# Two graph-attention layers with experts and a recurrence: the graph cast to bytes by DRAM-to-DRAM transfers, in place of int32 loads and casts on GpSimd

## The chip, the cores and the metric

The kernel runs on one core of a Trainium2 chip, a trn2. A core has four compute engines: TensorE (PE; its weight loads are shown as PEld), VectorE (DVE), ScalarE (ACT) and GpSimd (POOL). Each takes its own queue of instructions in order. A fifth queue, SyncE (SP), issues transfers. Sixteen transfer engines, shared by all queues, move the data. Transfers are issued from SP, ACT or POOL. Engines and transfers wait for each other through semaphores.

The metric is the device time of the whole program in microseconds (us). Less is better.

## What is computed

There are 3327 tokens of 256 features, and a dense graph `adj` of 3327 x 3327 int32 values, each 0 or 1. Only the parts around the change are shown in full:

```python
# layer 0: attention over the graph, 2 heads of 128
W3h = (h @ W3.T + b3).reshape(n, HEADS, C)
s1, s2 = ...                        # two scores for each token and head
e = leaky_relu(s1[:, None, :] + s2[None, :, :], 0.2)
e = where(adj[:, :, None] == 1, e, NEG)
att = softmax(e, axis=1)
h_prime = einsum('ijh,jhc->ihc', att, W3h)
# layer 0: the two best of 16 experts for each token
# layer 1: attention over the same graph, 1 head of 256, then elu
# layer 1: 30 steps of h + 0.01 tanh(h), h sigmoid(h), layernorm, h @ W.T + b
```

Both attention layers use the same graph. Each layer normalizes its input, and adds its result to it.

## The kernel before

**Tiles.** The 3327 tokens make NT = 26 tiles of up to 128, or PAIRS = 13 pairs. Token 2p + b of a pair stands at partition p of tile b of the pair. NP = 26 x 128 = 3328, so there is one place without a token: the last partition of tile 25. `rows(t)` gives the tokens of a tile: 128, and 127 for the last one.

**The graph in memory.** `adjT` holds the transposed graph as one-byte floats. [...]two neighbouring tokens travel together, and the tile is seen both as `adj_pairs` (two-byte) and as `adjT` (bytes). One tile of 128 rows of the graph fills the columns of `adjT` that belong to these 128 query tokens, for all tokens that they may attend to.

**Filling it** (`transpose_graph`, L240 to L264). For each of the 26 tiles, SP loads the rows in two halves of int32 into `raw` (three buffers), GpSimd casts each half to bytes in `bytes` (two buffers; L263, 52 casts in all), and a DMA transpose from SP (L264) writes them into `adj_pairs`. GpSimd also clears the column without a token (L262) and the last partitions of tile 25 (L260).

**The order of work at the start.** The weights of layer 0 are loaded by seven transfers from GpSimd (L319, L331). `project` (L130) goes over the tokens in seven groups (six of four tiles, one of two). For a group, `normalized` (L103) takes mean and variance on DVE, the reciprocal root on GpSimd (`rstd`, L114), and scales on DVE (`xn`, L116). Then, for two tiles at a time, PE transposes (L126), ACT copies (L127), PE multiplies by the weights (L141), and `split0` writes `wh`, the values that are to be averaged, and the scores. After `project` come, in program order, `transpose_graph` for all tiles, the loads of `gate_w` and `gate_b` from GpSimd (L365, L366), four small tables made by GpSimd (L368 to L377) and `before` (L378), which the routing to experts needs.

**Attention** (`attend`, L163). The query tiles are taken in groups: in layer 0 of 4, 6, 6, 6 and 4 tiles (`groups0`), in layer 1 of 3. One group and one head make a part, ten parts in layer 0. In a part the loop goes over the 26 tiles j of tokens that are attended to. In each step ACT makes `e` (L212), DVE adds and multiplies by the bytes of the graph (`pT`, L217), and PE multiplies `pT` by `wh[:, j]` for each tile of the group (L222, each matmul as two instructions in the trace). `wh` has a last column of ones, so the row sums come out of the same product. When a part is done, `close` divides (L195, L384) in the steps of the next part, a bit in each step. After the second head, `route` (L391) of that group is worked off in the same manner: normalize (with `rstd` on GpSimd), write `x` to `acc` and the normalized rows to `table_x` in DRAM (L398, L399, issued by SP), multiply by `gate_w` on PE (L406), find the two best experts on DVE, and scatter places into lists with GpSimd (L473).

**Who sets the order.** The program's lines are put into the five queues by a planner when the program is built. It prefers earlier lines, and takes later ones where earlier ones, by its estimate, can't run yet. Each engine then works its queue in order, and stops at an instruction whose inputs have not arrived.

**After attention 0.** The experts run from about 500 us, layer 1 (which projects with the same `project`, L716) from about 920, and the 30 steps to the end.

Of the kernel before, what the change touches and what calls it, by code (L numbers as in the profile page):

```python
# [17 lines left out]
P = 128  # L18
# [9 lines left out]
def gat_moe_gat_recurrent_ffn(ctx: ExitStack, tc: tile.TileContext, a: dict, out: bass.AP):  # L28
    nc = tc.nc
    N, D = a["x"].shape  # L30
    KD = D // P
    NT = (N + P - 1) // P
    NP = NT * P
    PAIRS = NT // 2
    REST = N - 2 * P * (PAIRS - 1)
    assert NT % 2 == 0
    E = a["gate_w"].shape[1]
    HID = a["w1"].shape[2]
    FH = HID // P
# [7 lines left out]
    def rows(t):  # L47
        return P if t < NT - 2 else (REST + 1 - t % 2) // 2

    def spread(n):  # L50

        cut = n - n % 16
        return [r for r in ((0, cut), (cut, n)) if r[0] < r[1]]
# [41 lines left out]
    neg_half = const.tile([P, MOST], F32, name="neg_half")  # L95
    nc.vector.memset(neg_half, -0.5)

    def load(name, shape, src, q=None):
        t = const.tile(shape, F32, name=name)
        (q or nc.sync).dma_start(t, src)  # L100
        return t

    def normalized(src, dst, scale=1.0):  # L103

        n = len(src)
        mv = small.tile([P, MOST, 2], F32, name="mv")
        for j in range(n):
            st = small.tile([P, 6], F32, name="st")
            nc.vector.bn_stats(st, src[j])
            nc.vector.bn_aggr(mv[:, j, :], st)  # L110
        ve = small.tile([P, MOST], F32, name="ve")
        nc.vector.tensor_scalar(ve[:, :n], mv[:, :n, 1], EPS, 1.0 / scale**2, op0=ALU.add, op1=ALU.mult)  # L112
        r = small.tile([P, MOST], F32, name="rstd")
        nc.gpsimd.tensor_tensor(r[:, :n], ve[:, :n], neg_half[:, :n], ALU.pow)  # L114
        for j in range(n):
            nc.vector.tensor_scalar(  # L116
                dst[j], src[j], mv[:, j, 0:1], r[:, j : j + 1], op0=ALU.subtract, op1=ALU.mult
            )
# [8 lines left out]
        nc.scalar.copy(hT, pt)  # L127
        return hT

    def project(wv, n_out, finish, work, ps, ps_p):  # L130

        for ts in groups:
            n = len(ts)
            xn = work.tile([P, G, D], F32, name="xn")
            normalized([x[:, t, :] for t in ts], [xn[:, j, :] for j in range(n)])
            for j0 in range(0, n, 2):
                hT = turned(xn[:, j0 : j0 + 2, :], work, ps)
                for j in range(2):
                    p = ps_p()
                    for k in range(KD):  # L140
                        nc.tensor.matmul(  # L141
                            p[:, :n_out], lhsT=hT[:, j, k, :], rhs=wv[:, k, :], start=(k == 0), stop=(k == KD - 1)
                        )
                    finish(ts[j0 + j], p)
# [92 lines left out]
    adj_pairs = graph.tile([P, PAIRS, NP], BF16, name="adjT")  # L237
    adjT = adj_pairs.bitcast(FP8).rearrange("p c (i b) -> p c i b", b=2)

    def transpose_graph(ts, pools):  # L240

        raw_p, cast_p = pools
        half = NP // 2
        for i in ts:
            pr = rows(i)
            b = cast_p.tile([P, NP], FP8, name="bytes")
            for lo in (0, half):
                real = min(half, N - lo)
                raw = raw_p.tile([P, half], I32, name="raw")
                for r0, r1 in spread(pr):  # L250
                    first = i // 2 * 2 * P + i % 2 + 2 * r0
                    nc.sync.dma_start(
                        raw[r0:r1, :real],
                        bass.AP(
                            tensor=a["adj"].tensor, offset=a["adj"].offset + first * N + lo,
                            ap=[[2 * N, r1 - r0], [1, real]],
                        ),
                    )
                if pr < P:
                    nc.gpsimd.memset(b[96:P, lo : lo + half], 0.0)  # L260
                if real < half:
                    nc.gpsimd.memset(b[:, lo + real : lo + half], 0.0)  # L262
                nc.gpsimd.tensor_copy(b[:pr, lo : lo + real], raw[:pr, :real], saturate=False)  # L263
            nc.sync.dma_start(adj_pairs[:, :, i * P : (i + 1) * P], b.bitcast(BF16), transpose=True)  # L264

# [10 lines left out]
    with ExitStack() as moe:  # L276
# [15 lines left out]
        with ExitStack() as st:  # L292
# [2 lines left out]
            keep = st.enter_context(tc.tile_pool(name="keep0", bufs=1))  # L295
            wh = keep.tile([P, NT, H, C + 1], F32, name="wh")
            sc = Scores(keep, H)
            gpools = (
                st.enter_context(tc.tile_pool(name="raw", bufs=3)),
                st.enter_context(tc.tile_pool(name="cast", bufs=2)),  # L300
            )
            ps = st.enter_context(tc.tile_pool(name="ps0", bufs=4, space=PSUM))
            ps_o = st.enter_context(tc.tile_pool(name="ps0o", bufs=2, space=PSUM))
            nc.vector.memset(wh[:, :, :, C : C + 1], 1.0)
# [4 lines left out]
            with ExitStack() as pre:  # L309
# [48 lines left out]
                    if t % G == G - 1 or t == NT - 1:  # L358
                        sc.finish(t - t % G, t + 1)

                project(wv, D + 2 * H, split0, work, ps, bank)
                transpose_graph(range(NT), gpools)


                nc.gpsimd.dma_start(gw, a["gate_w"].rearrange("(k p) e -> p k e", p=P))  # L365
# [25 lines left out]
            def route(ts):  # L391
# [3 lines left out]
                row = gate.tile([P, MOST, D], F32, name="row")  # L395
                normalized([x[:, t, :] for t in ts], [row[:, j, :] for j in range(n)])
                here = slice(t0 * P, (t0 + n) * P)
                nc.sync.dma_start(acc[here, :].rearrange("(t p) d -> p t d", p=P), x[:, t0 : t0 + n, :])  # L398
                nc.sync.dma_start(table_x[here, :].rearrange("(t p) d -> p t d", p=P), row[:, :n, :])  # L399
                yield  # L400
                pg = bank()[:, : n * E].rearrange("p (j e) -> p j e", e=E)
                for j0 in range(0, n, 2):
# [279 lines left out]
    with ExitStack() as st:  # L682
# [31 lines left out]
                sc.finish(t - t % G, t + 1)  # L714

        project(wv, D + 2, split1, work, ps, spot)  # L716

        run = st.enter_context(tc.tile_pool(name="edge2", bufs=3))
        rows_p = st.enter_context(tc.tile_pool(name="rows2", bufs=2))
# [146 lines left out]
```

## Time and profile before

| what | us |
|---|---|
| median of three runs | 2192.99 (2190.41 to 2193.59) |
| the profiled execution's own time | 2196.02 |
| its span, first to last instruction | 2194.3 |
| mean granted TensorE clock of it | 0.974 |

Times in the profile count from the start of the span. An engine's busy time leaves out waiting, and the issue of transfers is not counted as busy. The span and what lies around it make up the execution's own time (1.7 us more). In the profile's groups, a line has the place in the code, the engine and operation, what is written and read with the shape, the count, the busy time in us, the mean of one in ns, and after the second bar how long the engine stood idle just before these instructions, and what released it.

Milestones of this execution, from its timeline:

| event | us |
|---|---|
| first load of the graph issued (L252) | 11.3 |
| first matmul of `project` (L141) | 21.5 |
| first `e` of attention 0 (L212) | 65.1 |
| first matmul with `gate_w` (L406) | 144.6 |
| last cast of the graph (L263) | 236.0 |
| last division of attention 0 (L384) | 465.1 |

### The profile page before, as it was taken

Reading aid. Unit: us, or ns where it says so; the run is one execution under the profiler, and the core shown is the slowest. Engines: PE = TensorE matmul, PEld = TensorE weight load, DVE = VectorE, ACT = ScalarE, POOL = GpSimd, SP = SyncE. Lnnn points to the kernel's source line nnn. Section 1 sums busy time; section 2 is a strip of 40 time slices with the busy share of each in tenths; the row PEclk is TensorE's granted clock in tenths of the full one; section 3 lists DMA queues with packets and bytes.
Section 4 is the critical chain, followed back from the end, with each engine's and each line's share of the span. In section 5 each row is a group of like instructions: output and inputs, shape, how many; then the busy total and the mean of one; then the engine's idle time right before and its main releaser. Section 6 shows DMA issues by size and latency. Waiting matters only on the chain.

```text
span 2194.3 us, 31785 instructions
## 1 busy us (share of the span) xinstructions
PE 2024.3 (92%) x10912; PEld 1685.9 (77%) x10912; DVE 1574.8 (72%) x3948; ACT 1128.2 (51%) x1496; POOL 1030.5 (47%) x744
## 2 busy tenths in 40 slices
PE   5888898957999999869999999999999999999998
PEld 4788898954555555558888888888888888888887
DVE  6889876851121111155767589999999999999999
ACT  1655565721222222245665556666666666666664
POOL 5536402033444443310010027777777777777774
PEclk9989999977999999989999999999999999999999
DMA  9969400015666666320000000000000000000003
GB/s 283 305 209 234 119 15 16 30 39 142 175 186 172 195 177 157 84 82 8 15 8 15 8 32 1 1 1 1 1 1 1 1 1 1 1 1 1 1 1 106
DMA packets 124905, 155.08 MB, mean 71 GB/s; under 512 B 51561, under 2 KB 94637, under 8 KB 124745
## 3 DMA queue, kind: packets, MB, share of 16 engines
q1 hardware_dynamic: 109241, 133.12, 19.8%
q0 software_dynamic: 15360, 19.51, 5.0%
q8 instruction: 87, 1.43, 0.3%
q14 instruction: 73, 0.60, 0.1%
q10 hardware_dynamic: 144, 0.43, 0.0%
HBM read 170.95 MB, written 22.89 MB: 88 GB/s over the span
## 4 chain that ended last, share of the span: by engine, by line
PE 54%; DVE 18%; DMA 11%; issue 8%; POOL 4%; ACT 3%; SPq 2%; another core or an unknown queue 0%; POOLq 0%; DVEq 0%; ACTq 0%
PE po L801 20%; PE acc L222 15%; DVE x L806 5%; DMA raw<-in_adj_dram 5%; PE pa L620 4%; PE pb L620 4%; DVE stats L793 4%; PE po L651 4%; DMA ew<-in_w_dram 4%; PE pt L795 3%; ACT zT L797 3%; DVE v L768 2%; DVE v L767 2%; POOL bytes L263 2%; POOL lists L473 2%
## 5 line engine op out<-in xcount | busy, mean ns | idle before, releaser
L801 PE MATMUL po<-wc,zT 128*128 128x256 f32 x3120 | 705.3, 383 | 22.5 <-ACT zT L797 21.1
L801 PEld LDWEIGHTS po<-wc,zT 128*128 128x128 f32 x3120 | 582.9, 190 | 125.2 <-ACT zT L797 50.8
L222 PE MATMUL acc<-wh,pT 128*128 128x129 f32 (+1 forms) x4056 | 627.9, 316 | 32.1 <-DVE pT L217 27.3
L222 PEld LDWEIGHTS acc<-wh,pT 128*128 128x128 f32 x4056 | 575.5, 195 | 78.5 <-DVE pT L217 36.8
L217 DVE SCALAR_TENSOR_TENSOR pT<-e,part,adjT 128x384 f32<-128x384 f32 (+3 forms) x494 | 417.8, 856 | 152.2 <-PE acc L222 134.9
L212 ACT ACTIVATE e<-rb,minus,full 128x384 f32<-128x384 f32 (+3 forms) x494 | 398.6, 823 | 236.5 <-DVE pT L217 212.9
L787 POOL TENSOR_TENSOR th<-th,x 128x1024 f32<-128x1024 f32 (+1 forms) x210 | 460.5, 2211 | 42.8 <-ACT th L785 37.6
L797 ACT COPY zT<-pt 128x1024 f32<-128x1024 f32 (+1 forms) x210 | 199.4, 949 | 334.2 <-PE pt L795 334.2
L806 DVE SCALAR_TENSOR_TENSOR x<-po,rr,bb 128x256 f32<-128x256 f32 x780 | 323.4, 475 | 0.3 <-PE pt L795 0.3
L776 POOL TENSOR_TENSOR rr<-v,neg_half 128x4 f32<-128x4 f32 (+1 forms) x210 | 203.3, 968 | 216.1 <-DVE v L772 216.1
L793 DVE BATCH_NORM_STATS2 stats<-z 128x6 f32<-128x256 f32 x780 | 282.2, 413 | 0.2 <-ACT z L788 0.2
L114 POOL TENSOR_TENSOR rstd<-ve,neg_half 128x4 f32<-128x4 f32 (+3 forms) x28 | 30.7, 1096 | 433.4 <-DVE ve L112 343.6
L644 DVE TENSOR_TENSOR hid<-act,pb 128x512 f32<-128x512 f32 x67 | 46.1, 688 | 261.9 <-PE pb L620 261.9
L788 ACT ACTIVATE z<-th 128x1024 f32<-128x1024 f32 (+1 forms) x210 | 210.6, 1003 | 0.8 <-DVE stats L793 0.4
L785 ACT ACTIVATE th<-x 128x1024 f32<-128x1024 f32 (+1 forms) x210 | 199.2, 994 | 2.8 <-DVE x L116 1.9
L795 PE MATMUL pt<-ident,z 128*128 128x128 f32 x1560 | 191.6, 274 | 2.5 <-DVE high L727 2.5
L795 PEld LDWEIGHTS pt<-ident,z 128*128 128x128 f32 x1560 | 179.3, 141 | 14.9 <-issue 2.9
L654 POOL DMA_INDIRECT acc<-y,to x67 | 106.0, 1581 | 171.4 <-DMA acc<-y,to 89.4
L768 DVE SCALAR_TENSOR_TENSOR v<-v 128x4 f32<-128x4 f32 (+1 forms) x210 | 157.0, 748 | 0.0
L634 ACT ACTIVATE act<-pa 128x512 f32<-128x512 f32 x67 | 40.0, 597 | 218.7 <-PE pa L620 218.7
L620 PE MATMUL pa<-ew,hT 128*128 128x512 f32 x268 | 129.7, 607 | 17.2 <-DMA ew<-in_w_dram 16.1
L651 PE MATMUL po<-ew,hidT 128*128 128x256 f32 x536 | 126.9, 380 | 0.7 <-ACT hidT L640 0.7
(174 smaller groups left out, 1537.2 us busy)
## 6 DMA issues: line engine op xcount, KB each, us to landing
ew<-in_w_dram SPq DMA_DIRECT2D x201, 512.0 KB
raw<-in_adj_dram SPq DMA_DIRECT2D x25, 832.0 KB
raw<-in_adj_dram SPq DMA_DIRECT2D x25, 831.5 KB
x<-in_x_dram SPq DMA_DIRECT2D x6, 512.0 KB
x<-acc SPq DMA_DIRECT2D x6, 512.0 KB
kept<-x SPq DMA_DIRECT2D x8, 384.0 KB
old<-kept SPq DMA_DIRECT2D x6, 512.0 KB
out_dram<-x SPq DMA_DIRECT2D x6, 512.0 KB
```

Source lines behind the costliest of these rows:

```text
L212: nc.scalar.activation(e[:, : n * P], rb[:, : n * P], AF.Relu, scale=sc.full[:, j, h : h + 1], bias=sc.minus[:, j, h : h + 1],)
L217: nc.vector.scalar_tensor_tensor(pT[:, : n * P], e[:, : n * P], sc.part[:, j, h : h + 1], adjT[:, j // 2, ts[0] * P : (ts[-1] + 1) * P, j ...
L222: nc.tensor.matmul(po[c], lhsT=pT[:, c * P : (c + 1) * P], rhs=wh[:, j, h, :], start=(j == 0 and c % per_bank == 0), stop=(j == NT - 1), s ...
L620: nc.tensor.matmul(p, lhsT=hT[:, k, :], rhs=w[:, k, :], start=(k == 0), stop=(k == KD - 1))
L651: nc.tensor.matmul(po, lhsT=hidT[:, f, :], rhs=w3[:, f, :], start=(f == 0), stop=(f == FH - 1))
L787: nc.gpsimd.tensor_tensor(th[:, :n, :], th[:, :n, :], hs, ALU.add)
L788: nc.scalar.activation(z[:, :n, :], th[:, :n, :], AF.Silu, scale=1.0 / S)
L793: nc.vector.bn_stats(stats[:, j, :], z[:, j, :])
L795: nc.tensor.transpose(pt[:, j, k, :], z[:, j, k * P : (k + 1) * P], ident)
L797: nc.scalar.copy(zT[:, :n, :, :], pt[:, :n, :, :])
L801: nc.tensor.matmul(po[:, j, :], lhsT=zT[:, j, k, :], rhs=wc[:, k, :], start=(k == 0), stop=(k == KD - 1),)
L806: nc.vector.scalar_tensor_tensor(x[:, ts[0] + j, :], po[:, j, :], rr[:, j : j + 1], bb, op0=ALU.mult, op1=ALU.add)
```

## The change

The graph is cast by the transfers. For each pair of tiles, `cast_graph` takes a tile in DRAM of 256 rows of bytes, and GpSimd issues transfers from the int32 graph in DRAM to it, in pieces of at most 2048 columns: two for a pair, and four for the last pair, 28 in all. The generator gives control back after each pair. `project` got a new argument `aside`, and asks it for two pairs behind the `normalized` of each group. `transpose_graph` then issues two DMA transposes for a pair from SP, which read every second row from DRAM. There are 26 transposes as before.

The column without a token is not cleared any more: the pieces read one element past the row's end, which is the first of the next row, and the row of `wh` that it meets is multiplied by 0 instead. `real` is a column of ones with a 0 in the last partition, and it scales tile 25 of `wh`, its ones included, in both layers. The graph's last rows without a token are filled with zeros from SP, from a tile that is there already. The writes of `acc` and `table_x` are issued from ACT instead of SP. The buffers `raw` and `cast` and the unused function `load` go.

```diff
+    real = const.tile([P, 1], F32, name="real")
+    nc.gpsimd.iota(
+        real, pattern=[[0, 1]], base=rows(NT - 1), channel_multiplier=-1, allow_small_or_imprecise_dtypes=True
+    )
+    nc.vector.tensor_scalar(real, real, 0.0, None, op0=ALU.is_gt)
...
-    def project(wv, n_out, finish, work, ps, ps_p):
+    def project(wv, n_out, finish, work, ps, ps_p, aside=iter(())):
...
             normalized([x[:, t, :] for t in ts], [xn[:, j, :] for j in range(n)])
+            for _ in range(2):
+                next(aside, None)
...
-    def transpose_graph(ts, pools):
-
-        raw_p, cast_p = pools
-        half = NP // 2
-        for i in ts:
-            pr = rows(i)
-            b = cast_p.tile([P, NP], FP8, name="bytes")
-            for lo in (0, half):
-                real = min(half, N - lo)
-                raw = raw_p.tile([P, half], I32, name="raw")
...
-                if pr < P:
-                    nc.gpsimd.memset(b[96:P, lo : lo + half], 0.0)
-                if real < half:
-                    nc.gpsimd.memset(b[:, lo + real : lo + half], 0.0)
-                nc.gpsimd.tensor_copy(b[:pr, lo : lo + real], raw[:pr, :real], saturate=False)
-            nc.sync.dma_start(adj_pairs[:, :, i * P : (i + 1) * P], b.bitcast(BF16), transpose=True)
+    def cast_graph(zero, made):
...
+        last = N - 1 - 2 * P * (PAIRS - 1)
+        for c in range(PAIRS):
+            b = dram.tile([2 * P, NP], FP8, name=f"graph{c}")
+            first = 2 * P * c
+            pieces = [(0, 2 * P, N + 1)]
+            if c == PAIRS - 1:
+                pieces = [(0, last, N + 1), (last, last + 1, N)]
+                nc.sync.dma_start(b[last:, :], zero[: 2 * P - last, : NP // 4].bitcast(FP8))
+            for r0, r1, n in pieces:
+                for lo in range(0, n, 2048):
+                    hi = min(n, lo + 2048)
+                    nc.gpsimd.dma_start(
+                        b[r0:r1, lo:hi],
+                        bass.AP(
+                            tensor=a["adj"].tensor, offset=a["adj"].offset + (first + r0) * N + lo,
+                            ap=[[N, r1 - r0], [1, hi - lo]],
+                        ),
+                    )
+            made.append(b)
+            yield
+
+    def transpose_graph(c, b):
+
+        for i in range(2):
+            nc.sync.dma_start(
+                adj_pairs[:, :, (2 * c + i) * P : (2 * c + i + 1) * P],
+                b.bitcast(BF16).rearrange("(p i) n -> i p n", i=2)[i], transpose=True,
+            )
...
-                project(wv, D + 2 * H, split0, work, ps, bank)
-                transpose_graph(range(NT), gpools)
+                in_bytes = []
+                casting = cast_graph(zero, in_bytes)
+                project(wv, D + 2 * H, split0, work, ps, bank, casting)
+                assert len(in_bytes) == PAIRS
+                nc.vector.tensor_scalar(wh[:, NT - 1], wh[:, NT - 1], real[:, 0:1], None, op0=ALU.mult)
+                for c, b in enumerate(in_bytes):
+                    transpose_graph(c, b)
...
-                nc.sync.dma_start(acc[here, :].rearrange("(t p) d -> p t d", p=P), x[:, t0 : t0 + n, :])
-                nc.sync.dma_start(table_x[here, :].rearrange("(t p) d -> p t d", p=P), row[:, :n, :])
+                nc.scalar.dma_start(acc[here, :].rearrange("(t p) d -> p t d", p=P), x[:, t0 : t0 + n, :])
+                nc.scalar.dma_start(table_x[here, :].rearrange("(t p) d -> p t d", p=P), row[:, :n, :])
...
         project(wv, D + 2, split1, work, ps, spot)
+        nc.vector.tensor_scalar(wh[:, NT - 1], wh[:, NT - 1], real[:, 0:1], None, op0=ALU.mult)
```

More of the change, by code (lines that the diff above doesn't have):

```diff
@@ L35, in gat_moe_gat_recurrent_ffn @@
     REST = N - 2 * P * (PAIRS - 1)
-    assert NT % 2 == 0
+    assert NT % 2 == 0 and N == NP - 1
     E = a["gate_w"].shape[1]
@@ L96, in gat_moe_gat_recurrent_ffn @@
     nc.vector.memset(neg_half, -0.5)
[L98 to L101, printed above, removed]
+    real = const.tile([P, 1], F32, name="real")
[3 more added lines that the diff above has]
+    nc.vector.tensor_scalar(real, real, 0.0, None, op0=ALU.is_gt)
     def normalized(src, dst, scale=1.0):
@@ L238, in gat_moe_gat_recurrent_ffn @@
     adjT = adj_pairs.bitcast(FP8).rearrange("p c (i b) -> p c i b", b=2)
-    def transpose_graph(ts, pools):
-        raw_p, cast_p = pools
-        half = NP // 2
-        for i in ts:
-            pr = rows(i)
-            b = cast_p.tile([P, NP], FP8, name="bytes")
-            for lo in (0, half):
-                real = min(half, N - lo)
-                raw = raw_p.tile([P, half], I32, name="raw")
[L250 to L253, printed above, removed]
+    def cast_graph(zero, made):
[12 more added lines that the diff above has]
+                        b[r0:r1, lo:hi],
@@ L254, in transpose_graph @@
                         bass.AP(
-                            tensor=a["adj"].tensor, offset=a["adj"].offset + first * N + lo,
-                            ap=[[2 * N, r1 - r0], [1, real]],
-                        ),
-                    )
-                if pr < P:
-                    nc.gpsimd.memset(b[96:P, lo : lo + half], 0.0)
-                if real < half:
-                    nc.gpsimd.memset(b[:, lo + real : lo + half], 0.0)
-                nc.gpsimd.tensor_copy(b[:pr, lo : lo + real], raw[:pr, :real], saturate=False)
@@ L297, in gat_moe_gat_recurrent_ffn @@
             sc = Scores(keep, H)
[L298 to L301, printed above, removed]
             ps = st.enter_context(tc.tile_pool(name="ps0", bufs=4, space=PSUM))
```

## The prediction

> **What bounds the kernel now.** I read the slices of the page first, then the busy time by stretch inside layer 0, then the queue of GpSimd in order of time, last the transfers. The change lies in the first 465 us. Beyond, only one line of it runs, in layer 1.
>
> ```profile
> PE   5888898957999999869999999999999999999998
> POOL 5536402033444443310010027777777777777774
> DMA  9969400015666666320000000000000000000003
> ```
> A slice is 55 us. TensorE is nearly full throughout; the transfers are full in the first slices, where the graph comes in, and almost idle from slice 5 to 8. The question is whether this early load holds TensorE.
>
> ```profile
> 65.00:129.00 64.00, 55.82 (x446) 52.55 (x445) 59.71 (x63) 45.13 (x61) 30.23 (x26) 0.97 1.07 306
> ...
> 180.00:223.00 43.00, 38.28 (x325) 36.85 (x325) 41.62 (x38) 26.40 (x29) 24.21 (x19) 1.00 1.03 269
> ...
> 272.00:314.00 42.00, 37.15 (x304) 36.71 (x303) 28.91 (x40) 26.61 (x28) 4.94 (x5) 0.92 0.01 1
> 314.00:360.00 46.00, 44.23 (x389) 43.31 (x387) 36.21 (x85) 29.90 (x33) 10.05 (x9) 1.00 0.11 36
> 360.00:402.00 42.00, 36.57 (x293) 36.08 (x292) 27.95 (x38) 25.11 (x26) 4.52 (x5) 0.88 0.01 1
> 402.00:436.00 34.00, 31.27 (x270) 30.18 (x269) 29.34 (x88) 23.15 (x33) 2.50 (x2) 1.00 0.14 48
> 436.00:463.00 27.00, 24.05 (x204) 22.95 (x203) 18.53 (x32) 17.14 (x22) 12.64 (x12) 1.00 0.02 1
> ```
> The columns are length, then busy time of PE, PEld, DVE, ACT, POOL, then clock, DMA share and GB/s. The stretches are the parts of attention 0 (one group of rows, one head), cut where the first closing reciprocal (L195) of a part stands. While the graph comes in, DVE is the full engine (59.7 of 64, 41.6 of 43); afterwards it is not (28.9 of 42), and PE sets the pace. The same L217 is slower beside the casts, here in 160 to 240 and in 280 to 400 us:
>
> ```profile
> L217 DVE SCALAR_TENSOR_TENSOR pT<-e,part,adjT 128x768 f32<-128x768 f32 x48 | 67.6, 1438 | 4.7 <-PE acc L222 4.1 <-ACT e L212 0.6
> ...
> L217 DVE SCALAR_TENSOR_TENSOR pT<-e,part,adjT 128x768 f32<-128x768 f32 x74 | 75.0, 1015 | 26.3 <-PE acc L222 22.7 <-remote 1.7 <-ACT e L212 1.7
> ```
> No wait of DVE is for adjT: the graph itself is in time. That leaves what the new transfers do to GpSimd's queue and to what stands behind them:
>
> ```profile
> 17.54 1.01 POOL L114 TENSOR_TENSOR rstd<-ve,neg_half 128x4 f32<-128x4 f32 x1 [0.83 <-DVE ve L112]
> 18.50 0.10 POOL L262 MEMSET bytes<- 128x1 fp8e4 x1
> 18.54 0.76 POOL L365 DMA_DIRECT2D gate_w<-in_gate_w_dram  x1
> ...
> 22.75 1.04 POOL L114 TENSOR_TENSOR rstd<-ve,neg_half 128x4 f32<-128x4 f32 x1 [1.97 <-DVE ve L112]
> 23.77 1.56 POOL L263 CAST bytes<-raw 128x1664 fp8e4<-128x1664 int32 x1
> ```
> GpSimd's queue is not in program order: gate_w, written after all casts, was put before the first. But the four rstd of groups 0 to 3 (6.94, 12.57, 15.71, 17.54 us) have nothing between them, though the memset was ready: earlier lines that can run go first.
>
> ```profile
> SPq L252 <- DMA lists<-zero: 4.7, 1, 4.7
> SPq L252 <- DMA x<-in_x_dram: 2.5, 1, 2.5
> ```
> These are SP's own waits up to 30 us. The first load of the graph shares no data with lists<-zero, yet waits for it: that was the transfer eight places ahead. The transfers of SP and ACT take eight completion counters in turn, and one is taken again only when its last transfer has landed. GpSimd's have eight of their own: in the records its ninth transfer, gate_b, waits on the counter of the first, gw. So at most eight GpSimd transfers are under way, and the next one stops the whole in-order queue.
>
> **What the Trainium skill says.** "DMA: Bandwidth & Descriptors", section "SWDGE vs HWDGE vs iDMA": a transfer that casts can be issued from GpSimd only; no run shows one yet. Its section "Queues, rings and completion order": each transfer engine takes the descriptors of one ring in order; nothing in the trace contradicts it. Its section "Why a DMA increments its semaphore by 16 and not by 1": the number of engines is the largest divisor up to 16 of the slowest dimension, with an exception for some GpSimd copies; 254 rows would give 2. The trace doesn't show this case. "SBUF — State Buffer", section "Who interferes with whom": a DVE instruction with two SBUF inputs contends with a GpSimd instruction that reads SBUF; the trace agrees, 1438 against 1015 ns.
>
> **Removed: 52 casts on GpSimd.** What they cost is L217's slowing. I compare parts of equal kind: parts 0 and 1 took 64 us; parts 8 and 9 took 61, of which 5 are the route of six tiles (part 6 against part 7, 46 to 42), while the final part closes 2 us earlier: 58, so 6 won. Part 2 took 51, like part 6 with its 46: 5 won, some of it clock (0.87 there). Part 3: 43 against 42, 1. Part 4: 49 against 46, 3. Together 15 us. No more, because PE's 1.37 us a step (12 matmuls of 114 ns) is next in line.
>
> **Added: 28 casting transfers, and their pace.** A pair of tiles is 3.41 MB of int32. From below, the cast costs what the plain load costs. In 40 to 120 us the engines were full:
>
> ```profile
> DMA packets 23165, 24.43 MB, mean 305 GB/s; under 512 B 20252, under 2 KB 20252, under 8 KB 23158
> ...
> q1 hardware_dynamic: 23158, 24.34, 106.6%
> ...
> adjT<-bytes SPq DMA_TRANSPOSE x12
> ```
> Twelve tiles in 80 us, transposes included: 13.3 us a pair. From above: over the whole span GpSimd's own queue moved 19.51 MB in 5.0% of 16 engines' time, 178 GB/s, where SP's moved 133.12 MB in 19.8%, 306. At 178 the cast of a pair takes 19.1 us instead of 11.1, 21.3 with its transposes. I take 15: the results (0.85 MB a pair) are written to DRAM and read again. It is an estimate, near the lower end, because pieces of 8 KB are as long as today's loads, unlike the 1 KB rows of that queue.
>
> **The wait this puts into project.** Two pairs, four transfers, are issued behind each group's rstd. By the order of the lines, the seventh rstd stands behind 24 casts. With eight under way, it can run only when 16, eight pairs, have landed. Their bytes begin at about 12 us (gaT, one of the seven weight transfers ahead, landed at 11.2, and x keeps the engines full until then): 12 + 8 x 15 = 132, plus 2 for two issues of 0.8 and the rstd itself, 134. In before it ended at 31.9 and PE wanted its group at about 58. From there: two L116 of 0.41, then transposes, copy, matmuls and row factors as in before (last L126 at 60.15, first e of attention at 65.07): 1 + 5. Attention starts at 140 instead of 65: +75. Groups 3 to 5 wait likewise, inside this sum. Behind the waiting transfers on GpSimd stand the later rstd, then gate_w, gate_b, the iotas and `before`. PE stands behind rstd through xn.
>
> **gate_w.** It is issued behind the casts, so it lands behind them too: 12 + 13 x 15 = 207. PE needs it here:
>
> ```profile
> 144.63 1.73 PE L406 MATMUL bank<-gate_w,hT 128*128 128x16 f32 x8
> ```
> that is 80 us into attention, 72 without the casts' slowing: 140 + 72 = 212. It just arrives, so it adds nothing as long as attention is late by as much.
>
> **Transposes.** Same count on SP, now behind casts alone; pair 1 lands at about 45, pair 4 at 90, both before attention. Source in DRAM instead of SBUF: inside the 15.
>
> **Writes of acc and table_x on ACT.** Ten issues of 0.36 us, hidden: L212 is busy 26.6 of 42. ACT waits for row there, when PE waits for the same row (11.8 us in six waits of L126). 0; should each hold ACT for a whole chain of 3 us, +15. The counters could make them wait for a late transpose too; in the range.
>
> **Masks, iota, memset of zero rows.** Two DVE multiplications of 0.4 us on tile 25 alone, whose matmul is the last of 26; one 0.2 us iota. 0.
>
> **Sum** against the profiled execution (2196.02; span 2194.3): + 75 - 15 = 2256. The median of the runs is 3 lower: 2253.
>
> **Rivals.** B: the planner puts all rstd ahead of the waiting casts (as it did put them ahead of gate_w). Project ends at 63 as today, but gate_w still lands at 207 and PE stops at L406 at about 137: +70 - 15, 2248; with 13.3 a pair, 2223. For it: the rearranged queue above. Against: casts are written earlier than the next rstd and need nothing.
> C, the faster one: neither wait bites. If gate_w goes ahead of the casts, or the gate's matmuls are put late enough in PE's queue, and the rstd are free, only the 15 us remain: 2178. It decides at gate_w landing before 137 + 15 = 152: above it the gain is spent. For it: gate_w moved ahead once. Against: at 330 GB/s without any transposes 13 pairs need 134 us from 12 on, so behind the casts it cannot be.
> D: the casts are slower. At 21.3 a pair the seventh rstd runs at 184 and attention starts at 190: +125 - 15, 2303. If the last pair's 254 rows run on two engines, 2.1 MB at 2 x 19 GB/s last 54 us, gate_w lands near 257 and PE waits 45 more: 2298 with A, 2330 and more with both. For it: the divisor rule; against: the exception beside it.
>
> **Numbers.** A, the forecast, 2253, chance 0.40, its own range 2233 to 2285; B 0.15; C 0.15; D 0.30. All but C are slower. About 0.2% (4 us) is what can be told from no change; C falls into it seldom: faster 0.14, same 0.03, slower 0.83. The range 2174 to 2325 takes in C and most of D, and leaves out some 0.15.
>
> **What would show it.** Right: in the GpSimd queue rstd of groups 4 to 6 after 60 us with casts ahead of them; the first e near 140; 28 cast issues stretched to 150 us; L217 at 0.75 and 1.0 us from the start; PE idle before L126 in project. B: first e at 65 and a long wait of PE at L406. C: neither, first e at 65 and part lengths of 29 and 42. Wrong in size: cast landings apart by other than 15 us a pair. The forecast fails if GpSimd's transfers don't stop its queue, or the queue has rstd ahead of them.

## The result, and the profile after

The changed kernel takes 2221.16 us, median of four runs (2217.87 to 2228.81), beside 2192.7 for the kernel before: 1.0136 times as long, interval 1.0108 to 1.0165. On a second chip the ratio was 1.0156 (1.0113 to 1.0198). The forecast was 2253 with a range of 2174 to 2325: slower is right, but it said +60 us and the chip says +28.

The page of the kernel after, its slices:

```profile
PE   4559989984999999959999999999999999999998
...
POOL 3101020233434444320010017777777777777774
...
DMA  9993000013676766430000000000000000000003
```

TensorE is about half idle in slices 0 to 2, where it was busy for 80% or more from slice 1 on. GpSimd has lost the casts that stood in slices 0 to 4. The milestones, before and after:

| event | before, us | after, us |
|---|---|---|
| last `rstd` of `project` starts | 31.2 | 88.1 |
| first `e` of attention 0 | 65.1 | 102.8 |
| first `pT` of attention 0 | 65.9 | 132.8 |
| last `pT` of attention 0 | 461.5 | 490.3 |
| end | 2194.3 | 2216.2 |

Attention starts 66.9 later and is 38.1 shorter; what comes after it is 6.9 shorter, which sums to the 21.9 between the two spans. Why the late stages differ by 6.9 isn't known (nearly all of it lies in the experts). These are two single executions, and the one after is the fastest of its four, so the sum is a little below the 28 of the medians.

Two waits, not one, make the late start. The waits of the kernel after in its first 140 us (engine, line, what it waited for; us in total, times, longest):

```profile
POOL graph L260 <- DMA graph<-in_adj_dram: 73.9, 20, 5.3
ACT hT L129 <- PE bank L128: 58.7, 13, 20.7
DVE xn L118 <- POOL rstd L116: 36.6, 3, 13.0
DVE pT L221 <- DMA adjT<-graph: 30.4, 1, 30.4
...
PE acc L226 <- DVE pT L221: 29.2, 1, 29.2
```

The first and third line are the forecast's chain: GpSimd stands before a cast 20 times until an older one has landed, and DVE waits for the `rstd` queued behind. GpSimd's queue in order of time (start, length, then the idle time before the instruction and what ended it) shows it:

```profile
84.13 0.55 POOL L260 DMA_DIRECT2D graph<-in_adj_dram  x1 [4.76 <-DMA graph<-in_adj_dram]
87.57 0.55 POOL L260 DMA_DIRECT2D graph<-in_adj_dram  x1 [2.89 <-DMA graph<-in_adj_dram]
88.13 0.73 POOL L116 TENSOR_TENSOR rstd<-ve,neg_half 128x2 f32<-128x2 f32 x1
92.89 0.63 POOL L260 DMA_DIRECT2D graph<-in_adj_dram  x1 [4.04 <-DMA graph<-in_adj_dram]
...
110.52 0.76 POOL L378 DMA_DIRECT2D gate_w<-in_gate_w_dram  x1 [4.80 <-DMA graph<-in_adj_dram]
```

From 84.13 to 92.89 one pair goes by: 8.8 us, where the forecast had 15. The fourth line of the waits is one it did not have: DVE has nothing else to do from 102.4 on, the first `e` is there at about 103.6, and `pT` stands, 30.4 us in all, for the transposed graph. The transposes were starved. The transfers of the kernel after, first in 64 to 118 us, where they overlap the casts, then in 135 to 174, when the casts are done (queue: packets, MB, share of 16 engines; q0 is GpSimd's, q1 here the transposes'):

```profile
q0 software_dynamic: 3345, 5.22, 96.6%
q1 hardware_dynamic: 3345, 0.84, 11.6%
```

```profile
q1 hardware_dynamic: 30521, 7.67, 114.7%
...
adjT<-graph SPq DMA_TRANSPOSE x19
```

3345 packets to 3345: the engines moved as many packets of one queue as of the other, as they would if each queue got one in turn, and a cast's packet is as long as ten of a transpose's (a mean of 265 ns against 25 in the packet records). A transpose has 1664 packets of 256 bytes, 104 on each engine if they are spread evenly, so 104 turns of some 0.26 us are 27 us. SP's queue has the same: the first five issues last 10.9, 28.3, 26.7, 26.8 and 13.6 us, and the rest some 2 us each. By the packet records the first four transposes ended at 55.8, 83.1, 110.5 and 131.2 us.

### The profile page after: what moved, and what is told of

Its sections match the earlier page's. It is cut to its first block, busy times and chain, and to the rows that moved or that the text cites. A ratio compares the mean times of both kernels' runs of the same rounds, so it can differ in the third digit from the quotient of the medians.

```text
span 2216.2 us, 31645 instructions
## 1 busy us (share of the span) xinstructions
PE 2014.4 (91%) x10912; PEld 1680.7 (76%) x10912; DVE 1526.5 (69%) x3951; ACT 1131.2 (51%) x1496; POOL 955.3 (43%) x693
## 4 chain that ended last, share of the span: by engine, by line
PE 63%; issue 9%; DVE 6%; DMA 5%; ACT 4%; POOL 3%; SPq 1%; ACTq 0%; POOLq 0%; DVEq 0%
PE po L815 28%; PE acc L226 15%; PE pa L633 4%; PE pb L633 4%; PE po L664 4%; PE pt L809 4%; DMA ew<-in_w_dram 4%; ACT zT L811 4%; POOL lists L486 2%; DVE x L820 1%; DVE stats L807 1%; PE pu L652 1%; DVE pT L221 1%; PE acc L145 1%; DVE v L782 1%
## 5 line engine op out<-in xcount | busy, mean ns | idle before, releaser
L226 PE MATMUL acc<-wh,pT 128*128 128x129 f32 (+1 forms) x4056 | 612.4, 313 | 44.4 <-DVE pT L221 36.3
L226 PEld LDWEIGHTS acc<-wh,pT 128*128 128x128 f32 x4056 | 566.8, 193 | 84.0 <-DVE pT L221 38.6
L221 DVE SCALAR_TENSOR_TENSOR pT<-e,part,adjT 128x384 f32<-128x384 f32 (+3 forms) x494 | 380.1, 775 | 185.5 <-PE acc L226 126.6
L801 POOL TENSOR_TENSOR th<-th,x 128x1024 f32<-128x1024 f32 (+1 forms) x210 | 461.5, 2217 | 42.8 <-ACT th L799 38.2
```

Of the source, the lines that this page charges most:

```text
L221: nc.vector.scalar_tensor_tensor(pT[:, : n * P], e[:, : n * P], sc.part[:, j, h : h + 1], adjT[:, j // 2, ts[0] * P : (ts[-1] + 1) * P, j ...
L226: nc.tensor.matmul(po[c], lhsT=pT[:, c * P : (c + 1) * P], rhs=wh[:, j, h, :], start=(j == 0 and c % per_bank == 0), stop=(j == NT - 1), s ...
L801: nc.gpsimd.tensor_tensor(th[:, :n, :], th[:, :n, :], hs, ALU.add)
```

## The experiments

Theory 1: the start is set by transposes that take turns with the casts; the `rstd` behind the casts is hidden beneath it; the gain is DVE freed from GpSimd's casts. Rivals: the `rstd` alone sets the start; the source in DRAM makes the transposes slow; the shorter attention has another cause.

### All rstd ahead of the casts

```diff
+        for k, ts in enumerate(groups):
+            known[k] = statistics([x[:, t, :] for t in ts], 1.0, first)
+        for _ in aside:
+            pass
...
-            for _ in range(2):
-                next(aside, None)
```

> The changed kernel with the seven rstd of layer 0 ahead of the casts; casts and transposes as they are. Theory of the prediction (the wait of rstd behind the casts sets the start of attention): project ends near 63 us, attention starts some 37 us earlier than the 102.8 of the changed kernel, total about 2184. Rival (the transposes set it: each takes 27 us while casts flow, and the four of the first group land at 132): project ends near 63, but the first pT stays at 130 to 135 us, total within 5 us of the changed kernel, 2221.

2202.44 us, 1.0159 (1.0142 to 1.0176) of the kernel before on that chip: by this ratio no better than the change itself (and 6 us below the change with its writes on SP, 2208.89, which ran on the same chip). The first `e` is back at 65.2, but the first `pT` comes at 135.5. Its waits up to 160 us:

```profile
ACT e L226 <- DVE pT L231: 71.2, 4, 68.9
DVE pT L231 <- DMA adjT<-graph: 70.8, 1, 70.8
```

The whole 37 us that the `rstd` had cost went into the wait for the graph, 30.4 before and 70.8 now (the transposes also started 3 us later). The wait that the forecast was built on exists, and hid beneath a longer one.

### The same with casts in pieces of 512 columns

```diff
-                for lo in range(0, n, 2048):
-                    hi = min(n, lo + 2048)
+                for lo in range(0, n, 512):
+                    hi = min(n, lo + 512)
```

> As e1_rstd_ahead, with pieces of 512 columns in place of 2048. If a transpose is slow because each of its 256-byte packets waits for one packet of a cast (104 packets an engine, times one cast packet), its issue falls from 27 to 9 to 13 us while casts flow, the four tiles of the first group land at 70 to 80 us, and the total falls by 35 to 55 us against e1_rstd_ahead. If transposes are slow beside casts for another reason (the bytes moved, or the source in DRAM), they stay near 27 us and the total does not fall.

2193.05 us, 1.0111 (1.0094 to 1.0128): 9 us less than with the long pieces, where 35 to 55 had been expected. The first `pT` does move, from 135.5 to 78.1: a cast's packet has at most a quarter of the bytes (98 ns in place of 322), and a transpose beside casts takes 9 to 12 us. Its transfers in 40 to 60 us:

```profile
q0 software_dynamic: 3296, 1.52, 90.9%
q1 hardware_dynamic: 3297, 0.83, 31.8%
```

One for one again, but 3297 packets, two transposes, now go through in 20 us instead of 54. The mean packet of a cast is now 92 ns in the records, and 104 turns of it are 9.6 us. So the price is the length of the other queue's packet, and the transposes' source in DRAM is not slow by itself. Most of the won time is lost again in 60 to 200 us:

```profile
ACT e L226 <- DMA adjT<-graph: 31.9, 1, 31.9
...
PE bank L134 <- DVE row L124: 29.5, 1, 29.5
...
DVE pT L231 <- DMA adjT<-graph: 13.6, 1, 13.6
```

The last transposes come later: 13.6 us at the start of group 1. The longer stop is at the first route, and what ends last there is on ACT (start, length, the idle time before it and what ended that):

```profile
168.52 1.04 POOL L117 TENSOR_TENSOR rstd<-ve,neg_half 128x4 f32<-128x4 f32 x1
180.07 0.40 ACTq L422 DMA_DIRECT2D acc<-x  x1
180.52 3.78 ACT L226 ACTIVATE e<-rb,minus,full 128x768 f32<-128x768 f32 x4 [31.93 <-DMA adjT<-graph]
181.58 1.02 DVE L231 SCALAR_TENSOR_TENSOR pT<-e,part,adjT 128x768 f32<-128x768 f32 x1 [29.42 <-ACT e L226]
182.52 1.38 DVE L124 TENSOR_SCALAR row<-x,mv,rstd 128x256 f32<-128x256 f32 x4
```

The write of `acc`, which the change issues from ACT, takes over the completion counter of a transpose that was issued at 175.2, and it went out at 180.07, when that transpose had landed (180.0). `e` stood behind the write in ACT's queue, DVE's `pT` behind `e`, and the normalized rows, for which PE waits 29.5 us, behind `pT`. The `rstd` of this route was late too: 98 cast issues in place of 28 occupy GpSimd's queue until 166, and it ran at 168.5 behind them. But it was done some 10 us before the write went out. In the change itself the last transpose is issued at 174.3 and the first of these writes at 188.8, so there they don't meet.

### GpSimd casts put back beside attention

The kernel after with 52 casts of the old size on GpSimd, written for the first four parts, 13 for each. In the trace 12 of them ran ahead of the first `pT` and the other 40 beside parts 0 to 2. They read a tile made for them, and nothing reads what they write.

```diff
+                if k < 4:
+                    nc.gpsimd.tensor_copy(ints[:, 0:1], rb[:, 0:1])
+                    for _ in range(13):
+                        idle = spare_p.tile([P, NP // 2], FP8, name="idle")
+                        nc.gpsimd.tensor_copy(idle, ints, saturate=False)
```

> The changed kernel with 52 casts of 128x1664 int32 to bytes on GpSimd again, of a constant tile, beside parts 0 to 3 of attention 0; nothing reads them. If attention 0 became 38 us shorter because VectorE no longer contends with the casts: L217's multiplication takes 1.1 and 1.4 us in these parts again and the total grows by 20 to 38 us. If it became shorter for another reason (TensorE's clock after the idle start): it grows by less than 8.

2250.45 us (2249.04 to 2252.71), 1.0375 of the kernel before. Attention 0, from its first to its last `pT`, lasts 388.9 us, where the two other kernels on that chip whose start is like the change's took 346.6 and 339.1. So 42 to 50 us come back with the casts, and they come back by DVE: between 130 and 250 us `pT` of 512 columns took a mean of 1414 ns, in the kernel after 750. One of the parts in question (length, then busy time of PE, PEld, DVE, ACT, POOL, granted clock, transfers):

```profile
176.10:212.60 36.50, 29.63 (x212) 27.33 (x213) 34.14 (x36) 22.27 (x27) 21.29 (x11) 0.91 0.04 9
```

DVE is busy 34.1 of 36.5 and PE 29.6, with the transfers at rest (0.04): neither loads nor casts by transfers are needed for the slowing. The same part took 24.4 in the kernel after.

Not all of it is the price that the kernel before paid. In part 2 twelve of the casts came in one unbroken run:

```profile
253.25 19.53 DVE L223 SCALAR_TENSOR_TENSOR pT<-e,part,adjT 128x768 f32<-128x768 f32 x1
253.70 18.26 POOL L504 CAST idle<-ints 128x1664 fp8e4<-128x1664 int32 x12
```

One `pT`, which takes 1.0 us without casts beside it, took 19.5 while they ran. In the kernel before, where the casts wait for loads, the longest took 3.1. Parts 0 and 1, where casts and `pT` mostly alternate, took 80.4 us in place of 51.1 (the change with its writes on SP, the same chip): 29 us for 27 casts. That is the fairer price, some 1.1 us a cast.

### Writes of acc and table_x back on SP

```diff
-                nc.scalar.dma_start(acc[here, :].rearrange("(t p) d -> p t d", p=P), x[:, t0 : t0 + n, :])
-                nc.scalar.dma_start(table_x[here, :].rearrange("(t p) d -> p t d", p=P), row[:, :n, :])
+                nc.sync.dma_start(acc[here, :].rearrange("(t p) d -> p t d", p=P), x[:, t0 : t0 + n, :])
+                nc.sync.dma_start(table_x[here, :].rearrange("(t p) d -> p t d", p=P), row[:, :n, :])
```

> The changed kernel with the writes of acc and table_x issued from SP again. Theory: they are hidden on ACT, so the total stays within 3 us. Rival: they hold ACT at each of the five routings, and the total falls by 5 to 15 us.

2208.89 us (2203.5 to 2214.22), 1.0189 (1.0162 to 1.0216) of the kernel before, where the change measured 1.0136 and 1.0156 on other chips. No gain is seen: in the change the writes cost ACT nothing that counts. (With the short pieces above they did.)

### A ring that was none

Three kernels beside a second measurement of the change. All have the `rstd` and the gate loads ahead of the casts, and a pool of two byte tiles in DRAM (three in the last), meant to let at most two pairs of casts be under way. The second and third also have the root of the route on DVE, and the writes on SP.

```diff
+    bytes_p = ctx.enter_context(tc.tile_pool(name="bytes", bufs=2, space=bass.MemoryType.DRAM))
...
-            b = dram.tile([2 * P, NP], FP8, name=f"graph{c}")
+            b = bytes_p.tile([2 * P, NP], FP8, name="graph")
...
             made.append(b)
+            transpose_graph(c, b)
             yield
```

> The changed kernel itself, on the same chip as the three kernels beside it, as their reference. Both theories: 1.0136 times the kernel before, as on the first chip (1.011 to 1.017).

> Seven rstd and the gate loads ahead of the casts, and the byte tiles in DRAM in a ring of two, so that the casts of a pair wait for the transposes of the pair two before it. Theory 1 (the 27 us of a transpose come from casts that share its engines packet by packet): with at most two pairs of casts under way the first transposes take under 12 us, the first e stands at about 65 and the first pT before 75. If the transpose is slow by itself, because its source is in DRAM, the first pT stays near 130. What both leave open is the route of group 0, whose rstd still stands behind casts in GpSimd's queue: the ring stretches the casts, so this rstd runs only when the last pair is issued, at about 160 to 185; PE wants it at about 138, so 20 to 45 us are lost there. Total: 0.995 to 1.01 times the kernel before.

> The ring as beside it, the rstd of the route on DVE by shift, magic constant and three Newton steps instead of GpSimd, and the writes of acc and table_x from SP as in the kernel before. Theory 1: start as in the kernel before (first e at 65, first pT under 75), attention 0 as short as the undisturbed parts of the earlier runs show (24, 40, 36, 43, 36, 43, 36, 33, 24 us from reciprocal to reciprocal), so the last pT falls at about 425 to 435 instead of 461: 0.982 to 0.988 times the kernel before. Rival (the lead is lost to something else in the queues, such as a DVE that now has the root to do or SP's queue stopped by the transposes): 0.995 or more.

> The same with a ring of three tiles: three pairs of casts may be under way beside a transpose. Theory 1: transposes of up to 20 us instead of about 10, the first pT at about 70 to 85, but the last transposes earlier; total within 0.5% of the ring of two. If casts slow transposes only through the total load of the engines and not by turns, the two rings show the same transposes.

The change again: 1.0156. The three: 1.0403 (1.0358 to 1.0449), 1.0366 (1.0325 to 1.0408), 1.0345 (1.0304 to 1.0386), far off the expectation, and by the fault of the kernels. The second of them on ACT, in order of time:

```profile
65.85 0.19 ACT L187 ACTIVATE part<-s 128x4 f32<-128x4 f32 x1
178.63 0.59 ACT L213 COPY rb<-bank 128x512 f32<-128x512 f32 x1 [112.59 <-DMA graph<-zero]
```

No cast waited for a transpose: the pool gave each of the 13 pairs a tile of its own, and the transposes took 11, 28, 27, 27 us as before. But with each pair's transposes now written right behind its casts, the little transfer that fills the last pair's missing rows with zeros stood in SP's queue behind 24 transposes. It reads `zero`, whose place `rb`, the first tile of attention, takes over. So attention waited 112.6 us for a transfer of two rows. The kernels say nothing about a ring. They show what an in-order queue does to whatever is put behind a slow stretch of it.

### A ring that is one

Two tiles written again and again, the last pair's own tile filled at the start; everything else as in the second kernel above.

```diff
+        ring = [dram.tile([2 * P, NP], FP8, name=f"graph{k}") for k in range(RING + 1)]
+        nc.sync.dma_start(ring[RING][last:, :], zero[: 2 * P - last, : NP // 4].bitcast(FP8))
         for c in range(PAIRS):
-            b = bytes_p.tile([2 * P, NP], FP8, name="graph")
+            b = ring[RING] if c == PAIRS - 1 else ring[c % RING]
```

> A ring that is one: two byte tiles, made once and written again and again, so that the casts of a pair wait for the transposes of the pair two before it (the last pair has its own tile, whose zero rows are filled at the start). With seven rstd and the gate loads ahead of the casts, the root of the route on DVE and the writes of acc and table_x from SP. Theory 1 (casts and transposes take turns packet by packet; the earlier kernel with this aim had thirteen tiles all the same, so its casts never waited): at most four cast transfers beside a transpose, so a transpose takes at most about 9 us, the time in which these casts end, and 2 us otherwise; first e at 65 to 70, first pT before 75, no stall at the start of group 1 or at the route; the casts end at about 200 instead of 131, beside attention. Attention 0 as long as where nothing of this kind stands beside it, 355 to 375 us, so the last pT at 425 to 445 instead of 461; total 0.982 to 0.99 times the kernel before. Rival (casts that run beside attention slow it by more than the GpSimd casts did, or a transpose stays at 27 us beside any cast): 1.0 or more.

> The same ring with three tiles: up to six cast transfers beside a transpose. Theory 1: the first transposes of up to 18 us, first pT at 70 to 90, total within 0.7% of the ring of two. If the pace of transposes doesn't hang on what is in flight beside them, no difference in any transpose.

2143.77 us, 0.9863 (0.9824 to 0.9901) of the kernel before: faster than both given kernels. With three tiles 2146.96, 0.9875 (0.9839 to 0.9911). The page of the ring of two:

```profile
PE   5999999849999999699999999999999999999998
...
DMA  9997000145767665300000000000000000000003
```

its waits from 60 to 440 us:

```profile
POOL graph L285 <- DMA adjT<-graph: 94.1, 8, 22.5
```

and the stretch from its first to its last `pT`, in the columns of the stretches above:

```profile
66.50:411.30 344.80, 335.12 (x2919) 329.87 (x2919) 284.57 (x584) 252.68 (x289) 57.98 (x58) 0.99 0.45 66
```

GpSimd now waits for transposes, as it should, and next to nobody waits for GpSimd (the longest such wait in this stretch is 3.7 us). The first `pT` stands at 66.5, where the kernel before had 65.9, and attention takes 344.8 us instead of 395.5 (on another chip), with PE busy 335. A transpose took up to 11.3 us with two tiles (9 had been expected) and up to 16.1 with three: more in flight beside it, longer. The first `pT` of the three tiles came at 66.9, earlier than expected, since the four transposes that it needs had landed by 63. The casts are issued from 19 to 161 us, mostly beside attention, and cost it nothing that shows: parts 0 to 3 took 124.0 us, and 127.0 in the kernel with all `rstd` ahead, whose casts were over before. (All of attention took 339.1 there, on another chip; parts 5 and 7, long after the casts, make that difference, see below.)

### The ring, with the root of the route on GpSimd

```diff
-                    known=statistics([x[:, t, :] for t in ts], vector=True),
+                    known=statistics([x[:, t, :] for t in ts], vector=False),
```

> The ring of two, with the root of the route on GpSimd as in both given kernels, where it now stands behind all casts in the queue. If GpSimd's queue holds it (the wait that the prediction counted for project, here with no transpose to cover it): PE stops at the route of group 0 at about 135 to 140 until the last casts are issued at about 190, 40 to 60 us, and the total is longer than with the root on DVE by that. If the root on DVE is worth nothing: equal.

2187.58 us (2184.04 to 2194.12), 1.005 (1.0037 to 1.0064): 44 us more than the ring with the root on DVE. The waits in 60 to 400 us:

```profile
POOL graph L285 <- DMA adjT<-graph: 98.0, 8, 24.5
...
PE bank L148 <- DVE row L138: 42.4, 3, 39.7
DVE row L138 <- POOL rstd L131: 42.1, 3, 39.6
```

This is the forecast's own wait, seen bare: a root of 1 us behind casting transfers, and PE stopped for 39.7 us.

### The root on DVE in the kernel before

The ring's other edits have to be told from the change: the kernel before, with its route's root on DVE by a shift, a constant and three Newton steps.

> The kernel before with the root of the route on DVE, nothing of the change: how much of the lead of the ring of two (0.9863 times the kernel before) has nothing to do with who casts. If it is the casts that left GpSimd: the kernel before waits for its four route roots 3.7 us on DVE and 6.8 us on PE in all, DVE takes some 2 us of extra small instructions at each route, so 0.995 to 1.003. If the root is most of the lead: 0.990 or less.

2182.9 us, 1.0025 (1.0012 to 1.0039). The root on DVE earns nothing by itself. What is left for the ring's lead is the casts that left GpSimd, with the loads and buffers that went with them. The profiled execution took 387.2 us from first to last `pT`. Its span is 40.6 us longer than that of the ring of two, and 39.6 of it lies in parts 0 to 4, where the casts on GpSimd stand. (The two ran on different chips, on which the kernel before has the same median within 0.3 us.)

## Why the prediction was right and wrong

The sum failed in two terms: the transposes, put at nothing where they hold the first `pT` for 30 us, and the gain, put at 15 where 38 came. The start as a whole looks right because two errors in it cancel.

**Queue, eight under way, order: right.** Four casts stand between one `rstd` of `project` and the next, each later cast waits for the one eight places ahead, and `gate_w` comes behind them all. The shift of the start by the `rstd` was predicted from this with the right formula.

**The pace, 15 us a pair: wrong.** It is 8.8. Put into "12 + 8 x 15 = 132, plus 2", that gives 12 + 8 x 8.8 + 2 = 84 for the seventh `rstd`; the trace has 88.1. The lower bound of 13.3 was no bound, because it came from a stretch in which loads and transposes shared the engines in full: by its packet records the loads held them for 65% of the time and the transposes for 41%, and 0.65 x 13.3 is 8.7 us. In the changed kernel only four transposes went through up to 131 us, and 22 came after. The casts were fast at the transposes' cost.

**"Transposes ... pair 1 lands at about 45, pair 4 at 90, both before attention ... inside the 15": the step that failed.** It treated two queues as one stream with one rate. Group 0 needs the first four transposes, and they were done at about 131. This gave 30 of the 67 us of the late start; with the `rstd` out of the way it gives all of it. So +75 stood close to +66.9 by luck: as the trace has it, 37.7 come from the `rstd` and 29 from the transposes. The forecast's wait for `rstd` was 37 us too long, and the wait for transposes was missing. In the kernel before the question did not arise, because loads and transposes shared one queue. The Trainium skill, "DMA: Bandwidth & Descriptors", section "Queues, rings and completion order", says that an engine goes round the queues that have work packet by packet. The forecast used what the section says on order within one ring, and passed over this. The 3345 to 3345 packets agree with it. By the page a packet can hold several descriptors, and the counts don't tell how many of the trace's packets make one turn. Which wait ends last would have been asked by pricing each stream's packets: 104 turns on an engine, each with one cast's packet of nearly 0.3 us in front.

**The gain, 15 us: wrong, and the larger error.** It was 38 in the two profiles. The mechanism, DVE beside GpSimd, held: with casts put back, 42 to 50 us came back, some 18 of them by the one `pT` that was shut out. The attention lines of whole kernels, before and then after (count, busy us, mean ns):

```profile
L217 DVE SCALAR_TENSOR_TENSOR pT<-e,part,adjT 128x768 f32<-128x768 f32 x156 | 176.9, 1145 | 45.4 <-PE acc L222 40.1 <-remote 2.6 <-ACT e L212 2.3
...
L217 DVE SCALAR_TENSOR_TENSOR pT<-e,part,adjT 128x512 f32<-128x512 f32 x104 | 94.3, 930 | 12.6 <-PE acc L222 8.0 <-ACT e L212 1.1 <-remote 0.7
```

```profile
L221 DVE SCALAR_TENSOR_TENSOR pT<-e,part,adjT 128x768 f32<-128x768 f32 x156 | 157.1, 1013 | 49.3 <-PE acc L226 34.8 <-remote 10.8 <-ACT e L216 3.6
...
L221 DVE SCALAR_TENSOR_TENSOR pT<-e,part,adjT 128x512 f32<-128x512 f32 x104 | 76.9, 746 | 42.3 <-DMA adjT<-graph 30.4 <-PE acc L226 3.3 <-ACT e L216 0.9
```

What failed is the yardstick, "I compare parts of equal kind". The parts 5 and 7 that stood for undisturbed ones took 42 us, and were themselves slow. The same two parts of the kernel with all `rstd` ahead:

```profile
305.20:341.40 36.20, 36.20 (x327) 36.20 (x326) 28.38 (x40) 27.48 (x28) 7.21 (x7) 1.00 0.01 2
384.10:419.50 35.40, 35.40 (x320) 35.40 (x319) 27.76 (x39) 26.35 (x27) 7.18 (x7) 1.00 0.01 2
```

36.2 and 35.4, with PE busy to the last. The kernel after has 35.8 in its part 3, which is of the same kind, but 42.3 and 40.5 in its own parts 5 and 7. In the kernel before, part 7 opens with pauses of up to 3.6 us between PE and DVE, and then this, in stretches of 4 us from 364:

```profile
364.00:368.00 4.00, 2.58 (x12) 2.28 (x11) 0.47 (x2) 0.64 (x1) 1.44 (x2) 0.50 0.01 1
368.00:372.00 4.00, 3.36 (x15) 3.36 (x16) 3.90 (x10) 2.85 (x3) 0.00 (x0) 0.50 0.00 0
```

The granted clock is 0.50. The Trainium skill, "TensorE: Matmul & The Clock Gate", section "Part 1: The HAM clock gate (the "warmup" mystery)", has a half-rate clock until PE has been busy for a while; the 0.50 agrees. The forecast held what would have caught it: its rows for these parts show clocks of 0.92 and 0.88 and PE busy 37 of 42, and its own 1.37 us a step gives 26 x 1.37 = 35.6 us, not 42. From part to part the gain of 38.1 falls as 31 on parts 0 to 4, where the casts had been, and 7 on the later ones, where pauses and slow clock differ between the two executions. On parts 0 and 1 together, 2, 3 and 4 the forecast had 6, 5, 1 and 3, and the profiles differ by 12, 7, 7 and 5.

The pauses don't go with the kernel. All four profiled executions on the chip of the kernel with all `rstd` ahead have 36.2 us in part 5 and 35.5 in part 7, the one with casts put back too. The ten others, the kernel before and the rings among them, have 38.1 to 44.9 and 38.4 to 44.4. So attention of one chip set against that of another can be off by some 10 us for this alone.

**gate_w: right that nobody waits, wrong in its time.** It landed at about 132 instead of 207, was first used at 196.6, and nobody waited. That is ahead of the 152 of rival C too, whose "behind the casts it cannot be" rested on 330 GB/s; the casts read at 387. "If the last pair's 254 rows run on two engines" did not come true: the last pair's casts landed by 131, on the pace of the others. (B at 13.3 a pair comes to 2226 by its own terms, not 2223.)

**Writes on ACT, masks, zero rows: right,** nothing of them shows in the change. "The counters could make them wait for a late transpose too" came true with the short pieces, for 31.9 us.

With the measured terms, the forecast's sum reads 2196 + 67 - 38 - 7 = 2218, the profiled execution's own time.

## What to carry to other kernels

Where two streams of transfers overlap, compare the lengths of their packets before adding up their bytes: here a stream of small packets got one turn for each long packet of the other. Shorter packets on the other side helped; what made the kernel faster was to limit what is in flight beside the small ones. A transfer that is issued from a compute engine can stop that engine, when the counter that it needs is held by a slow transfer of another queue. A time that one wait explains may hide a second of the same length; ask for each input of the first instruction when it is there. And before a part of a profile serves as the undisturbed yardstick, hold it against the bounding engine's own pace and its granted clock.

## What the runs showed of the hardware

- A DMA transpose of 128 x 3328 bytes takes some 2 us alone, 9 to 12 beside casting transfers with packets of mostly 512 bytes written, and 27 beside 2048 and 1280.
- Casting from int32 to bytes, DRAM to DRAM, ran at 3.41 MB read in 8.8 us, 387 GB/s; a packet of 2048 bytes written (8192 read) took 322 ns.
- The transfers of SP and ACT took their completion counters in turn from one set: a write from ACT stood until a transpose from SP had landed, and `e` behind it for 31.9 us.
- Beside GpSimd casts that alternated with it, DVE's `pT` of 512 columns took 2.05 us instead of 0.75; an unbroken run of 12 casts held one `pT` of 768 columns for 19.5 us instead of 1.0.
- PE ran at half its clock (0.50) for some 8 us after a pause of 3.4 us. Why such pauses come at the start of a part in the executions on some chips, and in none of the four on another, stays open.
